# A scale and an offset read by GpSimd as one value for two neighbouring channels

## The chip, the cores and the metric

The kernel runs on one core of a Trainium2 chip. The metric is the device time of one execution in microseconds (us), as the median of several runs. In the profile, PE is TensorE's matmuls and PEld its weight loads, DVE is VectorE, ACT ScalarE, POOL GpSimd and SP SyncE, which here only issues transfers.

## The reference

Two layers of the same kind follow each other on an image of 512 x 512 positions with 64 channels, all in float32. Cut to what matters:

```python
def _gn(v, G=32, eps=1e-5):                 # 32 groups of two channels
    g = v.reshape(B_, H_, W_, G, C_ // G)
    m = jnp.mean(g, axis=(1, 2, 4), keepdims=True)
    s = jnp.var(g, axis=(1, 2, 4), keepdims=True)
    return ((g - m) / jnp.sqrt(s + eps)).reshape(v.shape)

def conv_ref(x, ...):                       # x is _gn of the layer's input
    xn = _ln(x, norm_scale, norm_bias)      # over the 64 channels
    left  = (xn @ Wl + bl) * mask * sigmoid(xn @ Wlg + blg)     # 64 -> 128
    right = (xn @ Wr + br) * mask * sigmoid(xn @ Wrg + brg)
    out_gate = sigmoid(xn @ Wog + bog)
    out = _banded_ingoing(left, right, 4)   # out[i] = sum over |d| <= 4 of left[i+d, i] * right[i+d]
    out = _ln(out, out_norm_scale, out_norm_bias) * out_gate
    return out @ Wo + bo                    # 128 -> 64

x = x + conv_ref(_gn(x), layer 0)
x = x + conv_ref(_gn(x), layer 1)
```

The first norm of a layer, `_gn`, has one mean and one variance for each group of two channels, over all positions. So it is one multiplier and one summand for each of 32 groups, the same at every position.

## The kernel before

Before the first layer the kernel reads the whole input once and takes its statistics (`input_stats`). The statistics of the second layer's input come from sums that the first layer takes on the way (`mid_stats`). Both end in `group_affine`, on VectorE, which makes the norm's multiplier `ga` and summand `gb`. Both are tiles of 128 partitions x 64 channels, the same on every partition, with each group's value written twice, once for each of its channels.

The image is worked on in nine blocks of rows; 64 rows of a block lie on the partitions, twice, for the left and the right half of the columns. A unit is eight columns of a block: its input tile `z` has 128 partitions x 8 columns x 64 channels, which is 512 contiguous values on a partition. Each unit goes through these steps, among others:

- `load` brings `z` from memory, through the SP queue.
- `scale` multiplies `z` by `ga` and `move` adds `gb`, in place. Both run on GpSimd, but for a few units at each layer's start that VectorE takes (`which`).
- `inner` takes the statistics of the second norm (`sti`) on VectorE; `centre` subtracts its mean and `resc` multiplies by its root (`rs`), both on GpSimd, in place. Here one value serves all 64 channels of a position.
- `ztr` transposes `z` on TensorE, into the PSUM tiles named `banks`; `keep`, `proj`, `sig` and `right` make the right factor `RO` from it.
- `band` multiplies the rows of `RO` with the band matrix `A` on TensorE and `copy` puts the result back into `RO`. `A` is loaded by the SP queue from `left_of`, anew for each block of rows.
- `ost` takes the statistics of the output norm, `norm` makes `on` from `RO`, part of the time on GpSimd (marked `!` in the tables) and else on ScalarE; `turn`, `gate`, `tg`, `last` and `end` finish the unit, and `stp` stores it.

The order of all this is written out by hand in two tables, `FIRST` and `SECOND`, one for each layer. A table is one period of eight units, called a chunk here; a layer has 36 chunks, four for each block of rows. Instructions that are recorded this way keep the order of the program on each engine, and all have line L492 in the profile, so groups are told apart by tile names.

`mid(v, n)` makes a view of a tile that repeats all its values n times, with a step of zero outside; `last(v, n)` repeats each value n times, with a step of zero inside. The scale reads `ga` through `mid`, the second norm's steps read theirs through `last`:

```python
engine.tensor_tensor(u.z, u.z, mid(ga, JU), ALU.mult)                   # scaled: 8 times 64 values
en.gpsimd.tensor_tensor(u.z, u.z, last(u.rs, D), ALU.mult)              # rescaled: 8 values, 64 times each
```

Of the kernel before, what the change touches and what calls it, by code (L numbers as in the profile page):

```python
# [10 lines left out]
F32 = mybir.dt.float32  # L11
# [3 lines left out]
ALU = mybir.AluOpType  # L15
# [4 lines left out]
P = 128  # L20
# [4 lines left out]
JU = 8  # L25
# [101 lines left out]
def mid(v: bass.AP, n: int) -> bass.AP:  # L127

    p, c = v.shape
    return v.unsqueeze(1).broadcast_to([p, n, c])  # L130
# [28 lines left out]
def tile_two_banded_layers(  # L159
# [6 lines left out]
    nc = tc.nc  # L166
# [3 lines left out]
    G = D // 2  # L170
# [3 lines left out]
    const = ctx.enter_context(tc.tile_pool(name="const", bufs=1))  # L174
# [62 lines left out]
    def rsqrt(o: bass.AP, v: bass.AP, sm):  # L237


        p, n = v.shape  # L240
        t, u = sm.tile([p, n], F32, name="rsqrt_t"), sm.tile([p, n], F32, name="rsqrt_u")
        nc.vector.tensor_scalar(
            o.bitcast(I32), v.bitcast(I32), -0.5, float(0x5F3759DF), ALU.mult, ALU.add
        )
        for a, b, c in ((1.0, -10.0 / 3.0, 5.0), (0.0, -27.0 / 1024.0, 0.5625)):
            nc.vector.tensor_tensor(t, o, o, ALU.mult)
            nc.vector.tensor_tensor(t, t, v, ALU.mult)
            nc.vector.tensor_scalar(u, t, a, b, ALU.mult, ALU.add)
            nc.vector.tensor_tensor(u, u, t, ALU.mult)
            nc.vector.tensor_scalar(u, u, c, None, ALU.add)  # L250
            nc.vector.tensor_tensor(o, o, u, ALU.mult)
# [144 lines left out]

    ga = const.tile([P, D], F32, name="ga")
    gb = const.tile([P, D], F32, name="gb")
    bo = [const.tile([P, D], F32, name="bo0"), None]
    bo_col = const.tile([P, 1], F32, name="bo_col")  # L400

# [6 lines left out]
    def group_affine(mean: bass.AP, var: bass.AP, pool):  # L408

        ve = pool.tile([P, D], F32, name="g_ve")  # L410
        nc.vector.tensor_scalar(ve, var, GN_EPS, None, ALU.add)
        rsqrt(ga, ve, pool)
        nc.vector.scalar_tensor_tensor(gb, mean, -1.0, ga, ALU.mult, ALU.mult)

    def input_stats(meanwhile, afterwards):
        flat = x.rearrange("h w c -> (h w) c").rearrange("(p n) c -> p n c", p=P)
# [3 lines left out]
        with tc.tile_pool(name="gnx", bufs=3) as gx, tc.tile_pool(name="gns", bufs=1) as gs:  # L420
# [23 lines left out]
            for t in range(n_t):  # L444
# [30 lines left out]
                vc.rearrange("p (g t) -> p g t", t=2), last(vg, 2), 0.5 / P, None, mult  # L475
            )
            group_affine(mc, vc, gs)


# [39 lines left out]
    def load_near(src: bass.AP, u: Unit):  # L519
# [3 lines left out]
        for o0, n0, n1 in spans:  # L523
            for o, r, k, m in runs(n0, n1):
# [20 lines left out]
                for q, g0, g1, a in pieces:  # L545
                    if g0 < g1:
# [2 lines left out]
                            strided(src, a * D, (D, 1), (1, (g1 - g0) * D)),  # L549
                        )  # L550

    def scaled(u: Unit, engine):
        engine.tensor_tensor(u.z, u.z, mid(ga, JU), ALU.mult)

    def moved(u: Unit, engine):
        engine.tensor_tensor(u.z, u.z, mid(gb, JU), ALU.add)

    def inner_stats(u: Unit, st: bass.AP, k: int):

# [356 lines left out]
    def layer(src: bass.AP, dst: bass.AP, w: dict, stats: bool, then=None):  # L916
# [57 lines left out]
        def on_scale(n, t, alt, b):  # L974
            for u in inputs(t):
                scaled(u, which(u, alt))

        def on_move(n, t, alt, b):
            for u in inputs(t):
                moved(u, which(u, alt))  # L980
# [155 lines left out]
    def mid_stats(sm):  # L1136
# [28 lines left out]
        nc.vector.tensor_scalar(var, var, 0.0, None, ALU.max)  # L1165
        nc.vector.tensor_tensor(ev[:, :D], ev[:, :D], bo[0], ALU.subtract)
        group_affine(ev[:, :D], var, sm)


# [95 lines left out]
def build(arrays):  # L1265
    import concourse.bacc as _bacc

    nc = _bacc.Bacc("TRN2", target_bir_lowering=False, num_devices=1)
    aps = {}
    for name in _INS:  # L1270
        a = arrays[f"in_{name}_dram"]
        aps[name] = nc.dram_tensor(
            f"in_{name}_dram", a.shape, mybir.dt.from_np(a.dtype), kind="ExternalInput"
        ).ap()
    out = nc.dram_tensor("out_0_dram", aps["x"].shape, F32, kind="ExternalOutput").ap()
    layers = [{n: aps[f"L{i}_conv_{n}"] for n in _NAMES} for i in range(2)]
    with tile.TileContext(nc) as tc:
        tile_two_banded_layers(tc, aps["x"], layers, out)
    return nc
# [10 lines left out]
```

## Time and profile before

| | |
|---|---|
| median of 3 runs | 4331.73 us (4329.06 to 4340.09) |
| span of the profiled execution | 4342.3 us |
| that span beside the median of the runs | 10.6 us longer; no time of that execution but its span is known |
| busy: PE, DVE, ACT, POOL | 3778.1, 3667.7, 3189.2, 3754.3 us |
| GpSimd's four instructions on `z`: by `ga`, by `gb`, by `sti`, by `rs` | 716.8, 715.7, 620.1, 614.9 us |
| GpSimd's `on<-RO,rs,nm` | 1129.1 us |

Busy time is time with an instruction at work; a share of the span is an average over stages. A group's row reads: line, engine, operation, output tile<-input tiles, their shapes, xcount, then busy us and mean ns of one, then the engine's idle time before them and what ended it. An idle time or a wait is put down to what came last.

### The profile page before, as it was taken

The numbers are of one execution on the slowest core, as the hardware profiler recorded it, in microseconds if no ns is written. First come the engines' busy times: TensorE is split into PE (matmuls) and PEld (weight loads), VectorE is DVE, ScalarE is ACT, GpSimd is POOL, SyncE is SP. The second block draws the span as 40 slices with busy tenths as digits, with TensorE's granted clock in tenths as the row PEclk, the third lists the DMA queues.
The fourth block names the chain that finished last, engine by engine and source line by source line (L and its number), as shares of the span: only waits on it lengthen the run. The fifth ranks groups of instructions, "written<-read, shape, count | busy, mean of one in ns | idle before, by whom it ended". The sixth has DMA issues, their size and how long they took to land.

```text
span 4342.3 us, 223298 instructions
## 1 busy us (share of the span) xinstructions
PE 3778.1 (87%) x94986; PEld 3263.8 (75%) x94986; DVE 3667.7 (84%) x9911; ACT 3189.2 (73%) x5976; POOL 3754.3 (86%) x4962
## 2 busy tenths in 40 slices
PE   0169899999898999999995889898989899989998
PEld 0058787878787878888874778787878787878786
DVE  8988787878787888888877788898989898989897
ACT  0048787878787877777773778787878787878787
POOL 2379898989898999999956789898989898989894
PEclk9989999999999999999997999999999999999999
DMA  9844545454545454445434344445454545454533
GB/s 393 313 110 108 134 113 143 115 141 114 140 115 138 112 141 120 131 123 129 125 109 114 101 136 124 139 128 138 123 142 122 143 120 145 121 145 121 152 112 100
DMA packets 695719, 596.26 MB, mean 137 GB/s; under 512 B 138310, under 2 KB 549990, under 8 KB 692420
## 3 DMA queue, kind: packets, MB, share of 16 engines
q1 hardware_dynamic: 692212, 580.43, 47.1%
q8 instruction: 748, 12.26, 1.2%
q14 instruction: 247, 2.02, 0.2%
q0 software_dynamic: 2512, 1.56, 0.1%
HBM read 436.71 MB, written 149.74 MB: 135 GB/s over the span
## 4 chain that ended last, share of the span: by engine, by line
PE 46%; POOL 20%; DVE 11%; DMA 9%; SPq 7%; issue 6%; ACT 2%; POOLq 0%; DVEq 0%; ACTq 0%
PE banks L492 35%; POOL z L492 13%; PE bank L492 8%; SPq L492 7%; POOL on L492 6%; PE acc L492 2%; DVE RO L492 2%; DMA z<-in_x_dram 2%; DMA z<-mid_x 2%; DVE gn_st L492 2%; DVE sti L492 1%; DVE sto L492 1%; DVE XR L492 1%; DVE ZH L492 1%; DMA raw<-in_L_conv_Wl_dram 1%
## 5 line engine op out<-in xcount | busy, mean ns | idle before, releaser
L492 POOL TENSOR_SCALAR on<-RO,rs,nm 128x128 f32<-128x128 f32 x2520 | 1129.1, 464 | 157.1 <-PE banks L492 111.2
L492 ACT ACTIVATE on<-RO,nm,rs 128x128 f32<-128x128 f32 x2088 | 971.2, 499 | 106.6 <-PE banks L492 95.2
L492 PE MATMUL banks<-pack,ZT 64*128 64x128 f32 x9216 | 992.3, 287 | 24.1 <-DVE RO L492 13.7
L492 PE MATMUL banks<-pack,zT 64*128 64x128 f32 x9216 | 953.1, 279 | 1.8 <-ACT zT L492 1.0
L492 POOL TENSOR_TENSOR z<-z,ga 128x512 f32<-128x512 f32 x556 | 716.8, 1296 | 261.0 <-DMA z<-mid_x 117.7
L492 ACT ACTIVATE sg<-banks 128x512 f32<-128x512 f32 x1170 | 696.6, 596 | 296.7 <-PE banks L492 270.9
L492 PEld LDWEIGHTS banks<-pack,ZT 64*128 64x128 f32 x9216 | 781.9, 194 | 148.4 <-DVE RO L492 47.5
L492 DVE TENSOR_TENSOR RO<-banks,sg 128x512 f32<-128x512 f32 x1152 | 777.3, 682 | 113.3 <-ACT sg L492 76.6
L492 DVE BATCH_NORM_STATS2 sto<-RO 128x6 f32<-128x256 f32 x2304 | 847.0, 413 | 5.2 <-ACT RO L492 4.0
L492 DVE SCALAR_TENSOR_TENSOR ZH<-banks,pack,ZH 128x896 f32<-128x896 f32 (+1 forms) x576 | 668.0, 1160 | 186.3 <-PE banks L492 155.4
L492 PEld LDWEIGHTS banks<-pack,zT 64*128 64x128 f32 x9216 | 762.2, 194 | 3.5 <-ACT zT L492 2.3
L492 PEld LDWEIGHTS banks<-RO,A 64*64 64x64 f32 x36864 | 617.7, 136 | 159.8 <-DVE RO L492 50.8
L492 PE MATMUL banks<-RO,A 64*64 64x64 f32 x36864 | 694.2, 223 | 48.6 <-issue 20.2
L492 POOL TENSOR_TENSOR z<-z,gb 128x512 f32<-128x512 f32 x556 | 715.7, 1293 | 3.3
L492 ACT COPY RO<-banks 128x1024 f32<-128x1024 f32 x540 | 539.8, 1008 | 194.5 <-PE banks L492 186.4
L492 PE MATMUL bank<-pack,ZH 128*64 128x64 f32 x18432 | 666.2, 226 | 15.7 <-DVE XR L492 5.6
L492 PEld LDWEIGHTS bank<-pack,ZH 128*64 128x64 f32 x18432 | 593.0, 139 | 76.7 <-issue 34.3
L492 ACT ACTIVATE ZH<-banks 128x896 f32<-128x896 f32 (+1 forms) x576 | 531.8, 930 | 142.6 <-PE banks L492 135.2
L492 POOL TENSOR_TENSOR z<-z,rs 128x512 f32<-128x512 f32 x586 | 614.9, 1059 | 19.7 <-DVE rs L492 19.4
L492 POOL TENSOR_TENSOR z<-z,sti 128x512 f32<-128x512 f32 x586 | 620.1, 1072 | 7.6 <-DVE sti L492 7.5
L492 DVE BATCH_NORM_STATS2 sti<-z 128x6 f32<-128x128 f32 x2344 | 505.6, 282 | 120.2 <-POOL z L492 118.0
L492 PE MATMUL banks<-ZT,pack 64*128 64x448 f32 (+1 forms) x2304 | 589.7, 584 | 9.8 <-DVE RO L492 5.5
(202 smaller groups left out, 4169.3 us busy)
## 6 DMA issues: line engine op xcount, KB each, us to landing
z<-in_x_dram SPq DMA_DIRECT2D x576, 128.0 KB
A<-left_of SPq DMA_DIRECT2D x576, 128.0 KB
z<-mid_x SPq DMA_DIRECT2D x576, 128.0 KB
gn_x<-in_x_dram SPq DMA_DIRECT2D x16, 4096.0 KB
XR<-in_x_dram SPq DMA_DIRECT2D x448, 112.0 KB
mid_x<-XR SPq DMA_DIRECT2D x448, 112.0 KB
XR<-mid_x SPq DMA_DIRECT2D x448, 112.0 KB
out_dram<-XR SPq DMA_DIRECT2D x448, 112.0 KB
```

Of the source, the lines that this page charges most:

```text
L492: return lambda *a, **k: tc.keep_in_program_order(f(*a, **k))
```

## The change

`group_affine` makes two more tiles, `ga2` and `gb2`, which hold one value for each of the 32 groups, by two copies on VectorE after `gb`. The scale and the offset then read those: a view with three dimensions after the partition, eight columns with step zero, 32 groups with step one, and two channels with step zero. The view of `z` is split the same way, which still is 512 contiguous values, and it is built as such. `ga` and `gb` stay.

```diff
+    ga2 = const.tile([P, G], F32, name="ga2")
+    gb2 = const.tile([P, G], F32, name="gb2")
...
         nc.vector.scalar_tensor_tensor(gb, mean, -1.0, ga, ALU.mult, ALU.mult)
+        for g, v in ((ga2, ga), (gb2, gb)):
+            nc.vector.tensor_copy(g, v.rearrange("p (g t) -> p g t", t=2)[:, :, 0])
...
+    def by_group(u: Unit, v: bass.AP, op, engine):
+
+        z = u.z.rearrange("p j (g t) -> p j g t", t=2)
+        engine.tensor_tensor(z, z, mid(v, JU).unsqueeze(3).broadcast_to([P, JU, G, 2]), op)
+
     def scaled(u: Unit, engine):
-        engine.tensor_tensor(u.z, u.z, mid(ga, JU), ALU.mult)
+        by_group(u, ga2, ALU.mult, engine)
 
     def moved(u: Unit, engine):
-        engine.tensor_tensor(u.z, u.z, mid(gb, JU), ALU.add)
+        by_group(u, gb2, ALU.add, engine)
```

The order of instructions is the same on every engine but for VectorE, which has the two copies at each layer's start. On VectorE at the first layer's start, from the summand on, before:

```order
L413 SCALAR_TENSOR_TENSOR gb<-gn_mc,ga 128x64
L492 TENSOR_TENSOR z<-z,ga 128x512
L492 TENSOR_TENSOR z<-z,gb 128x512
```

And now, where `ga_93` and `gb_94` are the tiles `ga2` and `gb2`, and lines further down have moved (L492 is L496):

```order
L415 SCALAR_TENSOR_TENSOR gb<-gn_mc,ga 128x64
L417 COPY ga_93<-ga 128x32
L417 COPY gb_94<-gb 128x32
L496 TENSOR_TENSOR z<-z,ga_93 128x512
L496 TENSOR_TENSOR z<-z,gb_94 128x512
```

The two copies stand between the summand and the first unit's scale, and nothing else has moved. GpSimd's first scale, which waited for `ga`, now waits for the copies.

## The prediction

> **What bounds the kernel now.** I read the head of the page first, then the stretches of single chunks, then the waits, and the groups by shape last, for prices.
>
> ```profile
> span 4342.3 us, 223298 instructions
> PE 3778.1 (87%) x94986; PEld 3263.8 (75%) x94986; DVE 3667.7 (84%) x9911; ACT 3189.2 (73%) x5976; POOL 3754.3 (86%) x4962
> PE 46%; POOL 20%; DVE 11%; DMA 9%; SPq 7%; issue 6%; ACT 2%; POOLq 0%; DVEq 0%; ACTq 0%
> ```
>
> Busy shares over the whole span name nobody: TensorE has 87%, GpSimd 86%, VectorE 84%. The chain that ended last (third line) has TensorE first and GpSimd second. So the question goes to single chunks. A chunk is eight units, one pass through the table of steps. I cut the stretches below where every eighth `z<-z,sti` of GpSimd starts. The columns are the length, then each engine's busy time.
>
> ```profile
> core 0: us, PE busy (x) PEld busy (x) DVE busy (x) ACT busy (x) POOL busy (x), PEclk, DMA share, GB/s
> 1027.10:1079.80 52.70, 51.17 (x1380) 44.97 (x1380) 46.13 (x125) 43.37 (x81) 52.62 (x71) 1.00 0.49 117
> 1132.50:1198.40 65.90, 54.95 (x1364) 48.44 (x1364) 45.30 (x119) 41.93 (x79) 52.74 (x71) 0.90 0.55 147
> 1478.50:1531.20 52.70, 51.16 (x1380) 45.00 (x1380) 46.06 (x125) 43.15 (x81) 52.62 (x71) 1.00 0.49 117
> 2151.10:2201.70 50.60, 50.37 (x1368) 44.43 (x1366) 42.69 (x106) 42.62 (x80) 41.47 (x62) 1.00 0.35 95
> 2528.00:2579.20 51.20, 50.74 (x1288) 43.73 (x1285) 48.58 (x131) 45.87 (x90) 50.17 (x65) 1.00 0.48 138
> 3072.80:3123.20 50.40, 49.54 (x1266) 42.87 (x1264) 47.05 (x127) 44.64 (x87) 50.15 (x66) 1.00 0.39 118
> 3225.30:3287.70 62.40, 52.88 (x1262) 45.53 (x1260) 47.24 (x126) 44.39 (x86) 50.18 (x66) 0.89 0.53 146
> 3718.20:3768.50 50.30, 49.27 (x1262) 42.48 (x1259) 46.74 (x126) 44.31 (x86) 50.02 (x65) 1.00 0.39 118
> ```
>
> In an ordinary chunk GpSimd is full: 52.62 of 52.70 us in the first layer, 50.02 of 50.30 and 50.15 of 50.40 in the second. It sets the period. TensorE is close behind, with 51.17 of 52.70 and 49.27 of 50.30: 1.5 us of slack a chunk in the first layer and 1.0 in the second. Its granted clock there is 1.00, so its busy time cannot shrink by a better clock. VectorE has 3.6 to 6.6 us of slack. Two chunks show what happens when TensorE is the bound: at 2151.10 us GpSimd has only 41.47 us of work and TensorE is busy 50.37 of 50.60, and at 2528.00 us it is 50.74 of 51.20. So a TensorE-bound chunk is its busy time plus 0.2 to 0.5 us.
>
> Every fourth chunk, where the next block of rows begins, is 62 to 66 us long. GpSimd's work is the same there; the rest is a stall.
>
> ```profile
> POOL z L492 <- DMA z<-mid_x: 117.7, 45, 14.0
> POOL z L492 <- DMA z<-in_x_dram: 107.1, 39, 5.5
> PE banks L492 <- POOL on L492: 120.3, 69, 5.8
> 3022.04 1.27 POOL L492 TENSOR_TENSOR z<-z,ga 128x512 f32<-128x512 f32 x1 [5.03 <-DMA z<-mid_x]
> 3009.94 1.15 SPq L492
> 3027.64 2.88 DMA z<-mid_x
> ```
>
> The first three lines are waits in all, times and the longest; the fourth is GpSimd in the stall at 3022 us; the last two are the first and the last piece of this part of the chain of waits. From 3009.94 to 3027.64 us, 17.7 us, the chain runs through the issuing of transfers on the SP queue, where the loads of `z` stand among those of `A`. A faster GpSimd does not shorten that piece.
>
> **What the change touches.** The order of instructions on all engines is the same but for four copies on VectorE. What changes is the second operand of the scale and the offset: 32 values, each read twice running, eight times over, where it was 64 values read once each, eight times over. The first operand and the result, `z`, stay 512 contiguous values. So nearly all hangs on the duration of one form. The nearest rows on GpSimd (busy us, mean ns, idle before):
>
> ```profile
> L492 POOL TENSOR_TENSOR z<-z,ga 128x512 f32<-128x512 f32 x556 | 716.8, 1296 | 261.0 <-DMA z<-mid_x 117.7 <-DMA z<-in_x_dram 107.1 <-PE banks L492 18.2
> L492 POOL TENSOR_TENSOR z<-z,gb 128x512 f32<-128x512 f32 x556 | 715.7, 1293 | 3.3
> L492 POOL TENSOR_TENSOR z<-z,rs 128x512 f32<-128x512 f32 x586 | 614.9, 1059 | 19.7 <-DVE rs L492 19.4
> L492 POOL TENSOR_TENSOR z<-z,sti 128x512 f32<-128x512 f32 x586 | 620.1, 1072 | 7.6 <-DVE sti L492 7.5
> L492 POOL TENSOR_TENSOR gn_s<-gn_s,gn_off 128x64 f32<-128x64 f32 x28 | 9.0, 320 | 2.1
> L492 POOL TENSOR_TENSOR gn_off<-gn_st 128x64 f32<-128x64 f32 x14 | 5.8, 414 | 40.6 <-DVE gn_st L492 40.6
> L492 POOL TENSOR_TENSOR gn_own<-gn_own,gn_st 128x64 f32<-128x64 f32 x14 | 4.7, 336 | 0.0
> L492 POOL TENSOR_SCALAR on<-RO,rs,nm 128x128 f32<-128x128 f32 x2520 | 1129.1, 464 | 157.1 <-PE banks L492 111.2 <-DVE nm L492 36.0 <-ACT acc L492 5.3
> masks.py:199 POOL TENSOR_SCALAR_AFFINE_SELECT ident<-ident 128x128 f32<-128x128 f32 x1 | 0.3, 323 | 0.1
> ```
>
> *Low end.* `z<-z,rs` and `z<-z,sti` have the same size, the same engine and the same contiguous `z`; their second operand repeats one value 64 times. They take 1059 and 1072 ns against 1296 and 1293. So repeating a value is worth up to 237 ns, and how far two repeats get of the way that 64 get is the unknown. *No gain:* 1296. *Above:* two rows have operands in runs of two. `gn_own<-gn_own,gn_st` reads its second operand as 32 runs of two, and takes 336 against the 320 of `gn_s`, all contiguous: 16 ns for 32 runs, 0.5 ns a run, and with 256 runs 128 ns on top of 1296, 1424 ns. `on<-RO` reads 64 runs of two, 1 KB apart, in 464 ns against the 323 of a contiguous one of that size: 2.2 ns a run, 564 ns for 256, 1860 ns. That row has another operation with two scalars read besides, so it is the farther.
>
> Between these I take the middle of 1296 and 1059, 1178 ns. The reason is in the `gn_` rows. With one operand strided the price is 16 ns, with both (`gn_off<-gn_st`, 414) it is 94. So the extra time seems to come where both operands go on to fresh memory together, not from either alone. `ga` and `z` now do so in step; with pairs, the second goes on half as often, so half of the 237 ns should go: 118 ns an instruction.
>
> [...]
>
> **The sum.** Per chunk 8 scales and 8 offsets: 16 × 118 ns = 1.89 us less on GpSimd. First layer: 52.62 − 1.89 = 50.73, below TensorE's 51.17, so TensorE sets the period: 51.17 + 0.35 (the middle of the two chunks above) = 51.5, a gain of 1.2 us. Second layer: 50.1 − 1.9 = 48.2, below TensorE's 49.4; 49.4 + 0.35 = 49.75 against 50.35, a gain of 0.6 us. A layer has 36 chunks; without the 8 at a change of block and some 3 at the ends, 25 are ordinary: 25 × 1.2 + 25 × 0.6 = 45 us. In the 16 chunks at a change of block all but the SP queue's piece is as elsewhere; two thirds of the mean gain of 0.9 us gives 16 × 0.6 = 10 us. Together 55 us. At a layer's end I count nothing (in the chunk at 2151.10 us GpSimd is not the bound), nor at its start, where ten such instructions in a row would be 1.2 us.
>
> The copies lie on the path at each layer's start, since all units wait for the scale:
>
> ```profile
> 213.01 0.22 DVE L413 SCALAR_TENSOR_TENSOR gb<-gn_mc,ga 128x64 f32<-128x64 f32 x1
> 213.06 1.29 POOL L492 TENSOR_TENSOR z<-z,ga 128x512 f32<-128x512 f32 x1 [17.66 <-DVE ga L251]
> 209.34 0.19 DVE L474 TENSOR_SCALAR gn_vc<-gn_vg 128x64 f32<-128x64 f32 x1
> 209.56 0.20 DVE L411 TENSOR_SCALAR g_ve<-gn_vc 128x64 f32<-128x64 f32 x1
> L492 DVE TENSOR_TENSOR z<-z,ga 128x512 f32<-128x512 f32 x30 | 33.9, 1144 | 6.3 <-DMA z<-mid_x 5.2 <-DMA z<-in_x_dram 1.1
> L492 DVE TENSOR_TENSOR z<-z,gb 128x512 f32<-128x512 f32 x30 | 31.2, 1050 | 0.2
> ```
>
> GpSimd starts right when `ga` is done, at 213.06. It will wait for `gb` (0.22 us) and, as bounded by the 0.19 and 0.20 us of 64-wide rows, two copies: 0.6 us a layer, 1.2 us in both. VectorE's own 60 scales and offsets change their operand too. L474 reads each value twice running, in 0.19 us, against 0.20 for the contiguous L411: no price either way. Nothing else is added, and nobody's queue order moves.
>
> So 55 − 1.2 = 54 us less. The profiled execution's span, 4342.3, is 10.6 us above the median of the runs, 4331.7; the difference is taken from the median: **4278 us**.
>
> How far this can be off while its mechanism holds: if the whole 237 ns went, TensorE would still be the bound, so the time is nearly the same; if TensorE packed closer than its busy time tells, GpSimd's 1112 instructions × 118 ns = 131 us would be the most, 4200. If TensorE's waits on ScalarE and VectorE grow as GpSimd's go, half is left, 4305. Its own range is 4240 to 4312.
>
> **The rivals.**
>
> *The form does not change its time (no change).* If GpSimd's price is per value fetched, with a run of two costing as much as two contiguous ones, it stays at 1296 ns and the time at 4332 + 1. The low row needs 64 repeats, and nothing shows what two are worth. It is also the outcome if the gain is there but TensorE, at 97 to 98% in ordinary chunks, gives none of its 1.0 to 1.5 us. Against: 1296 to 1059 is a step in just the property that the change uses.
>
> [...]
>
> *Runs of two cost more than they save (slower).* Place: the same 1112 instructions, in the engine that sets the period, so each ns is paid: 16 ns a chunk per ns, 1.1 us over the kernel. At 1424 ns, 128 × 1112 = 142 us more, 4474 us; at the far end, 1860 ns, 627 us more. It decides from 1296 + 12 ns on (12 × 1112 = 13 us). For it: `gn_own` is the nearest row with runs of two, and it is dearer than contiguous. Against: its runs are also strided, 12 bytes apart inside and 384 between, and the new ones lie side by side.
>
> **How the numbers follow.** Faster with TensorE as the new bound, 4278: 0.60. No change, by either way: 0.20. Slower: 0.20, most of it below 1424 ns, a twentieth at the far end. About 0.3%, 13 us, is what a measurement of this kernel can tell from no change. The range starts at 4235, leaving out a twentieth in which TensorE packs closer, and goes up to 4400, which holds no change and about the milder quarter of the slower cases (up to 60 ns an instruction); beyond it lie 0.15. As cases of both signs are in it, the likeliest one's own 4240 to 4312 stands beside it.
>
> **What would show it.** In the profile of the changed kernel: `z<-z,ga2` and `z<-z,gb2` near 1178 ns (right), at 1296 (first rival), above 1310 (second); `z<-z,rs` unchanged at 1059. In ordinary chunks GpSimd should show 1 us or more idle, first named as waiting for TensorE's `banks` or for `z` transfers, and TensorE within 0.5 us of the chunk's length, at 51.5 and 49.75 us. Chunks at a change of block should keep a stall of about 11 us. The prediction is wrong if GpSimd is faster and the chunks stay at 52.7 and 50.3, or if chunks get shorter than TensorE's busy time now.

## The result, and the profile after

The changed kernel takes 4286.2 us (median of 4 runs, 4281.05 to 4288.38) against 4335.9 for the kernel before (4 runs, 4329.06 to 4346.16). The ratio is 0.9886, with a 95% interval of 0.9870 to 0.9903: 1.1% faster, some 50 us. The two profiled spans differ by 4342.3 − 4286.6 = 55.7 us. The forecast was 4278.

The head of the page of the changed kernel, with the chain's shares by engine:

```profile
span 4286.6 us, 223301 instructions
PE 3756.5 (88%) x94986; PEld 3258.3 (76%) x94986; DVE 3657.6 (85%) x9915; ACT 3181.7 (74%) x5976; POOL 3620.0 (84%) x4962
PE 58%; DVE 12%; POOL 9%; DMA 7%; SPq 6%; issue 5%; ACT 2%; DVEq 0%; POOLq 0%; ACTq 0%
```

GpSimd's busy time fell by 134 us and its share of the chain from 20% to 9%; TensorE's rose from 46% to 58%. Where GpSimd's time went is seen in the groups by shape (the profile prints `ga` for `ga2`):

```profile
L496 POOL TENSOR_TENSOR z<-z,gb 128x512 f32<-128x512 f32 x556 | 651.5, 1177 | 3.3
L496 POOL TENSOR_TENSOR z<-z,ga 128x512 f32<-128x512 f32 x556 | 649.8, 1175 | 301.9 <-DMA z<-in_x_dram 135.3 <-DMA z<-mid_x 114.5 <-PE banks L496 20.0
L496 POOL TENSOR_TENSOR z<-z,sti 128x512 f32<-128x512 f32 x586 | 617.8, 1067 | 7.7 <-DVE sti L496 7.7
L496 POOL TENSOR_TENSOR z<-z,rs 128x512 f32<-128x512 f32 x586 | 611.9, 1053 | 20.9 <-DVE rs L496 20.5
```

The scale takes 1175 ns and the offset 1177, 121 and 116 ns less than before; the other two forms are as they were, within 6 ns. The stretches of single chunks, two of the first layer (the second one at a change of block), then three of the second (the last one at a change of block):

```profile
core 0: us, PE busy (x) PEld busy (x) DVE busy (x) ACT busy (x) POOL busy (x), PEclk, DMA share, GB/s
1466.50:1517.50 51.00, 49.90 (x1353) 44.18 (x1353) 45.55 (x122) 42.62 (x81) 50.70 (x71) 1.00 0.46 116
1127.50:1193.20 65.70, 54.83 (x1370) 48.49 (x1366) 44.92 (x117) 42.00 (x79) 50.64 (x70) 0.90 0.53 143
2624.00:2672.90 48.90, 48.84 (x1262) 42.52 (x1262) 46.91 (x127) 44.29 (x86) 48.16 (x66) 1.00 0.39 122
3464.10:3512.80 48.70, 48.60 (x1260) 42.27 (x1260) 46.57 (x126) 44.05 (x86) 48.09 (x65) 1.00 0.39 122
2772.70:2833.30 60.60, 51.05 (x1256) 43.97 (x1254) 46.85 (x126) 43.96 (x85) 48.30 (x66) 0.92 0.53 150
```

In the second layer's ordinary chunk TensorE is busy 48.84 of 48.90 us and 48.60 of 48.70, while GpSimd has 0.6 to 0.7 us to spare. In the first layer's chunk shown, GpSimd still has the larger busy time, 50.70 of 51.00, against 49.90 for TensorE.

A block of rows is four chunks. The means over eight blocks of each layer, from the starts of every eighth `z<-z,sti` in both traces, in us (for the last two rows the eight begin one block earlier, as those of the last block fall in the layer's end):

| chunk | layer 1 before | after | layer 2 before | after |
|---|---|---|---|---|
| at the change of block | 64.20 | 64.43 | 62.14 | 60.88 |
| the next | 52.81 | 51.60 | 50.34 | 49.02 |
| the one after | 52.77 | 51.73 | 51.18 | 49.87 |
| the last of the block | 54.73 | 54.63 | 51.08 | 49.73 |

Eight times the differences: 17 us less in the first layer, from two chunks of four; 42 us less in the second, from all four. Together they are 59 us; outside these chunks the execution became 59 − 55.7 = 3 us longer. Of the mean lengths in the second layer TensorE is busy 48.87 of 49.02, 49.16 of 49.87 and 49.20 of 49.73 us (before 49.39, 49.44 and 49.71), and GpSimd 48.2 of each. In the first layer's two chunks that became shorter, neither is full: TensorE is busy 50.70 of 51.60 and 50.94 of 51.73 us, GpSimd 50.75 and 50.76.

The waits in all, as before in us, times and the longest:

```profile
POOL on L496 <- PE banks L496: 139.9, 86, 7.3
POOL z L496 <- DMA z<-in_x_dram: 135.3, 44, 6.7
PE banks L496 <- POOL on L496: 119.3, 48, 5.7
POOL z L496 <- DMA z<-mid_x: 114.5, 52, 10.8
```

GpSimd's wait for the first layer's input grew from 107.1 to 135.3 us: that is the layer in which half of the chunks gave nothing back. The last row of `ga` on VectorE, in the kernel before and now, then the copies and GpSimd's first scale:

```profile
212.75 0.22 DVE L251 TENSOR_TENSOR ga<-ga,rsqrt_u 128x64 f32<-128x64 f32 x1
212.55 0.22 DVE L251 TENSOR_TENSOR ga<-ga,rsqrt_u 128x64 f32<-128x64 f32 x1
212.96 0.17 DVE L417 COPY ga<-ga 128x32 f32<-128x32 f32 x1
213.07 0.18 DVE L417 COPY gb<-gb 128x32 f32<-128x32 f32 x1
213.21 1.15 POOL L496 TENSOR_TENSOR z<-z,ga 128x512 f32<-128x512 f32 x1 [18.01 <-DVE ga L417]
```

`ga` was finished at 212.97 us and GpSimd's scale started at 213.06, 0.09 us later; now `ga` is finished at 212.77 and the scale starts at 213.21, 0.44 us later. So the copies cost 0.35 us here. The scale starts before the second copy is done (213.07 + 0.18 = 213.25): it waits for the first alone.

### The profile page after: what moved, and what is told of

Read it like the earlier page. It is cut to its first block, busy times and chain, and to the rows that moved or that the text cites. A ratio compares the mean times of both kernels' runs of the same rounds, so it can differ in the third digit from the quotient of the medians.

```text
span 4286.6 us, 223301 instructions
## 1 busy us (share of the span) xinstructions
PE 3756.5 (88%) x94986; PEld 3258.3 (76%) x94986; DVE 3657.6 (85%) x9915; ACT 3181.7 (74%) x5976; POOL 3620.0 (84%) x4962
## 4 chain that ended last, share of the span: by engine, by line
PE 58%; DVE 12%; POOL 9%; DMA 7%; SPq 6%; issue 5%; ACT 2%; DVEq 0%; POOLq 0%; ACTq 0%
PE banks L496 44%; PE bank L496 10%; POOL z L496 6%; SPq L496 6%; POOL on L496 3%; PE acc L496 3%; DVE sti L496 2%; DMA z<-in_x_dram 2%; DVE RO L496 2%; DVE sto L496 2%; DVE gn_st L496 2%; DMA z<-mid_x 2%; DVE XR L496 1%; DVE ZH L496 1%; ACT on L496 1%
## 5 line engine op out<-in xcount | busy, mean ns | idle before, releaser
L496 POOL TENSOR_SCALAR on<-RO,rs,nm 128x128 f32<-128x128 f32 x2520 | 1117.9, 456 | 193.3 <-PE banks L496 139.9
L496 ACT ACTIVATE on<-RO,nm,rs 128x128 f32<-128x128 f32 x2088 | 971.7, 499 | 108.4 <-PE banks L496 95.1
L496 PE MATMUL banks<-pack,ZT 64*128 64x128 f32 x9216 | 987.4, 287 | 24.4 <-DVE RO L496 15.3
L496 PE MATMUL banks<-pack,zT 64*128 64x128 f32 x9216 | 945.0, 279 | 2.2 <-issue 1.3
L496 POOL TENSOR_TENSOR z<-z,ga 128x512 f32<-128x512 f32 x556 | 649.8, 1175 | 301.9 <-DMA z<-in_x_dram 135.3
L496 ACT ACTIVATE sg<-banks 128x512 f32<-128x512 f32 x1170 | 696.1, 596 | 279.9 <-PE banks L496 253.8
L496 PEld LDWEIGHTS banks<-pack,ZT 64*128 64x128 f32 x9216 | 771.5, 194 | 148.4 <-DVE RO L496 49.6
L496 DVE TENSOR_TENSOR RO<-banks,sg 128x512 f32<-128x512 f32 x1152 | 777.6, 683 | 94.8 <-ACT sg L496 72.5
L496 DVE BATCH_NORM_STATS2 sto<-RO 128x6 f32<-128x256 f32 x2304 | 847.9, 413 | 6.7 <-ACT RO L496 2.6
L496 DVE SCALAR_TENSOR_TENSOR ZH<-banks,pack,ZH 128x896 f32<-128x896 f32 (+1 forms) x576 | 668.7, 1161 | 195.5 <-PE banks L496 163.2
L496 PEld LDWEIGHTS banks<-pack,zT 64*128 64x128 f32 x9216 | 754.0, 194 | 3.9 <-ACT zT L496 2.4
L496 PEld LDWEIGHTS banks<-RO,A 64*64 64x64 f32 x36864 | 617.2, 136 | 139.0 <-DVE RO L496 43.9
L496 PE MATMUL banks<-RO,A 64*64 64x64 f32 x36864 | 693.4, 223 | 32.3 <-issue 18.8
L496 PE MATMUL bank<-pack,ZH 128*64 128x64 f32 x18432 | 666.7, 226 | 12.5 <-DVE XR L496 5.6
L496 ACT COPY RO<-banks 128x1024 f32<-128x1024 f32 x540 | 540.2, 1008 | 173.6 <-PE banks L496 162.1
L496 POOL TENSOR_TENSOR z<-z,gb 128x512 f32<-128x512 f32 x556 | 651.5, 1177 | 3.3
L496 PEld LDWEIGHTS bank<-pack,ZH 128*64 128x64 f32 x18432 | 594.0, 139 | 72.9 <-issue 31.0
L496 ACT ACTIVATE ZH<-banks 128x896 f32<-128x896 f32 (+1 forms) x576 | 531.6, 929 | 135.2 <-PE banks L496 129.4
L496 POOL TENSOR_TENSOR z<-z,rs 128x512 f32<-128x512 f32 x586 | 611.9, 1053 | 20.9 <-DVE rs L496 20.5
L496 POOL TENSOR_TENSOR z<-z,sti 128x512 f32<-128x512 f32 x586 | 617.8, 1067 | 7.7 <-DVE sti L496 7.7
L496 PE MATMUL banks<-ZT,pack 64*128 64x448 f32 (+1 forms) x2304 | 587.3, 583 | 3.4 <-issue 1.2
L496 PE MATMUL banks<-ident,on 64*128 64x64 f32 x9216 | 461.7, 230 | 125.7 <-POOL on L496 119.3
```

Source lines behind the costliest of these rows:

```text
L496: return lambda *a, **k: tc.keep_in_program_order(f(*a, **k))
```

## The experiments

Two things were open: why the instruction got faster, and what limits the kernel now. The experiments ran on chips on which the kernel before took 4350 to 4354 us, so times are compared as ratios to it; the changed kernel's, 0.9886, is from the runs above, and it was not run on these chips.

### Why the instruction is faster

Three theories of the author's: V, every fresh value of the second operand costs; O, every new stretch of memory that it enters costs; J, this costs only where the first operand enters one at the same element. The prediction rested on J without showing it. How long a stretch would be, no run shows.

Pairs without the compact tiles:

```diff
-    ga2 = const.tile([P, G], F32, name="ga2")
+    ga2 = ga.rearrange("p (g t) -> p g t", t=2)[:, :, 0]
```

> The scale and the offset read pairs straight out of ga and gb: 32 values two apart (8 bytes), each read twice running; no compact tiles and no copies. So there are as few fresh values as in the changed kernel, but the second operand goes through as many bytes as before. If the price is for each fresh value of the second operand (theory V), GpSimd's instruction takes 1177 ns as in the changed kernel and the time is 4286. [...] If runs of two had a price of their own, hidden in the changed kernel, it is above 1296.

```profile
L494 POOL TENSOR_TENSOR z<-z,ga 128x512 f32<-128x512 f32 x556 | 714.7, 1293 | 271.6 <-DMA z<-in_x_dram 114.8 <-DMA z<-mid_x 110.0 <-DVE ga L251 32.4
```

1293 ns, as before; the ratio is 1.0002 (0.9991 to 1.0012). Reading half as many values is worth nothing; keeping them close together is what counts. V falls; O and J fit, as the operand goes through as many bytes as before. Runs of two have no price of their own either, since this form has them too.

The kernel before, its tiles moved by 8 bytes (`gb` likewise), so that by J, if a stretch is longer than that, the two operands no longer enter one at the same element:

```diff
-    ga = const.tile([P, D], F32, name="ga")
+    ga = const.tile([P, D + 8], F32, name="ga")[:, 2 : D + 2]
```

> [...] Theory J: the two never enter together, so the price is gone: 1059 ns, the level of z<-z,rs, and a time of 4275 to 4286, set by TensorE. Theories O and V: nothing changes for the second operand, 1296 ns and 4332.

```profile
L492 POOL TENSOR_TENSOR z<-z,ga 128x512 f32<-128x512 f32 x556 | 612.6, 1108 | 347.0 <-DMA z<-in_x_dram 160.2 <-DMA z<-mid_x 156.4 <-DVE ga L251 17.7
```

1108 ns from 1296, with the same values read in the same pattern, from another place. O falls, J fits, but for some 50 ns that stay above 1059. The ratio is 0.9891 (0.9865 to 0.9918): the whole gain of the change, without its tiles, copies and view.

The changed kernel, its tiles moved by 4 bytes (`ga2 = const.tile([P, G + 8], ...)[:, 1 : G + 1]`, and `gb2`), to the same end:

> [...] Theory J: 1059 ns, against 1177 unshifted; as TensorE sets the period already, the time falls by 10 us at most, 4275 to 4286. Theories O and V: 1177 ns and 4286.

```profile
L496 POOL TENSOR_TENSOR z<-z,ga 128x512 f32<-128x512 f32 x556 | 611.1, 1105 | 334.1 <-DMA z<-in_x_dram 155.6 <-DMA z<-mid_x 116.2 <-DVE ga L417 33.1
```

1105 ns from 1175: as J has it, with the same rest above 1059. The ratio is 0.9878 (0.9860 to 0.9896), no different from the changed kernel's, though each instruction is 70 ns shorter.

Each value for four channels (`"p (g t) -> p g t", t=4`, tiles of 16 values):

> Each value is read for four neighbouring channels (16 values instead of 32, the first of each four, so the first norm's result is another). All three theories: a quarter of the 237 ns is left, 1059 + 59 = 1118 ns. The time is set by TensorE: 4275 to 4286. If instead the step from 1296 to 1177 had another cause than the share of fresh values, such as the number of dimensions of the view, it stays at 1177.

```profile
L496 POOL TENSOR_TENSOR z<-z,ga 128x512 f32<-128x512 f32 x556 | 617.3, 1116 | 327.6 <-DMA z<-in_x_dram 156.3 <-DMA z<-mid_x 122.9 <-PE banks L496 27.2
```

1116 ns where 1118 was expected: in tiles that are not moved the price goes with the share of entries, all to 1296 ns, a half to 1175, a quarter to 1116. The ratio is 0.9887 (0.9864 to 0.9910).

The kernel before, moved by 4 bytes in place of 8 (`[:, 1 : D + 1]`):

> [...] Theory J as e2 left it: anything but together is free of the price, so 1107 ns as there. If the price fades with the distance between the two entries, it is between 1107 and 1296.

```profile
L492 POOL TENSOR_TENSOR z<-z,ga 128x512 f32<-128x512 f32 x556 | 611.7, 1107 | 331.3 <-DMA z<-in_x_dram 156.0 <-DMA z<-mid_x 133.3 <-DVE ga L251 32.4
```

1107 ns: one value's distance does as well as two. Its single run took 4298 us beside 4350, about the same ratio. What the last 45 to 50 ns are is not settled: if they were for the second operand's own entries, they should have halved from `e2` to `e3`, and they did not. Two things stay open with them. The three moved forms take 1105 to 1108 ns whatever they read, which also fits a flat time for any second operand that does not start where such a stretch does, with a price for its own entries in the other forms alone; a run with `z` moved as well would tell, and there is none. And under J the moves by 4 and 8 bytes show only that a stretch is longer than 8 bytes, not how long it is.

### What limits the kernel now

Half the edit (the offset reads `gb` as before):

```diff
-        by_group(u, gb2, ALU.add, engine)
+        engine.tensor_tensor(u.z, u.z, mid(gb, JU), ALU.add)
```

> Only the scale reads pairs; the offset reads gb as before. GpSimd then wins half, 8 x 118 ns = 0.95 us a chunk: 51.7 us of work in the first layer, 49.2 in the second, just at TensorE's 51.2 and 49.3. If TensorE takes over as the prediction has it, half of the edit brings most of the gain: 0.9 us a chunk in the first layer and 0.6 in the second, some 40 to 45 us with the chunks at a change of block, a ratio of 0.990. Rival: the time follows GpSimd's work all the way, and the whole edit is only worth 55 us because some of each saved us is lost in waits; then half the edit is worth half, 27 us, a ratio of 0.9937.

The ratio is 0.9937 (0.9922 to 0.9953), the rival's number to the digit. Up to half the edit the time still follows GpSimd's work, at the rate that the whole edit has.

All of it and more, one value for 64 channels:

```diff
-        engine.tensor_tensor(z, z, mid(v, JU).unsqueeze(3).broadcast_to([P, JU, G, 2]), op)
+        engine.tensor_tensor(u.z, u.z, last(v[:, :JU], D), op)
```

> The scale and the offset read one value for all 64 channels of a column, as rs is read (so the first norm's result is another). GpSimd: 1059 ns an instruction, 3.8 us less a chunk than before, twice the changed kernel's gain. If TensorE is the bound after the change, the time is that of the changed kernel or up to 10 us below: a ratio of 0.986 to 0.989. If GpSimd's work still sets it: 0.976.

```profile
L496 POOL TENSOR_TENSOR z<-z,ga 128x512 f32<-128x512 f32 x556 | 587.5, 1062 | 362.5 <-DMA z<-in_x_dram 173.0 <-DMA z<-mid_x 140.8 <-DVE ga L417 33.2
```

```profile
2630.60:2679.20 48.60, 48.59 (x1258) 42.23 (x1256) 46.67 (x126) 44.09 (x87) 46.42 (x66) 1.00 0.40 123
```

1062 ns an instruction and a ratio of 0.9883 (0.9867 to 0.9899): twice the saving on GpSimd, and nothing more for the kernel. In the chunk shown GpSimd has 46.42 us of work in 48.60, and TensorE 48.59. So the saving pays up to the changed kernel's level and stops there: GpSimd's work is no longer what limits the kernel.

More work for TensorE, first in the kernel before, then in the changed one:

```diff
-        for e in range(2):
+        for e in (0, 1) * (2 if o.at % NU == 3 else 1):      # in gates
```

> The kernel before, with the gate's matmuls (banks<-ZT,pack, four records in 0.85 us) done twice for one unit of eight, into the same bank with the same result: TensorE gets 0.85 us more a chunk. If GpSimd is the bound there and TensorE has 1.5 us of slack in the first layer and 1.0 in the second, this is hidden: 0 to 15 us, a ratio of 1.000 to 1.0035.

> The same 0.85 us more a chunk for TensorE in the changed kernel. If TensorE is the bound there, as the prediction has it, it is paid in the second layer's 36 chunks and in the half of the first layer's that had become shorter (the others wait for transfers): 36 x 0.85 + 18 x 0.85 = 46 us, a ratio of 0.9992 where the changed kernel has 0.9886. Rival, after the run without the seeds brought nothing: waits or transfers limit the changed kernel and TensorE still has slack; then as in the kernel before, 0 to 15 us, 0.989 to 0.992.

The changed kernel goes to 0.9985 (0.9970 to 1.0000), 0.0099 × 4350 = 43 us more, close to the 46 of a TensorE that is full. The kernel before goes to 1.0062 (1.0046 to 1.0077), 27 us more where 15 was the most expected: less of its slack was usable than busy times show. The same work costs more in the changed kernel, as it must if TensorE is nearer to its limit there; by the intervals the difference is 16 us, give or take 12. By the traces, 34 us of it lie in the second layer, where the chunk after a change of block is 49.60 us long with TensorE busy for 49.53.

Less work for TensorE, in both kernels (`seeded` not called, `end(outs[t], w, True)`):

> The kernel before without the second layer's seeding matmuls, bank<-pieces,ones, which add the output bias of both layers (left out here); the first matmul on the bank starts the sum instead. This takes TensorE 8 matmuls a chunk of 0.21 us each, 1.7 us in 36 chunks. If GpSimd is the bound of the kernel before, its chunks in the second layer stay at 50.3 us and the time falls by 5 us at most, a ratio of 0.999 or more. If TensorE were the bound, by 40 to 60 us.

> The changed kernel without the same matmuls. If TensorE is its bound, the second layer's chunks fall to what GpSimd needs, 48.15 + 0.15 = 48.3 us from 48.7 to 50, and those at a change of block by as much: 25 x 1.1 + 8 x 1 = 35 us below the changed kernel, a ratio of 0.980 to the kernel before, where the changed kernel has 0.9886. Rival: what limits the changed kernel is not TensorE's work but the waits between engines or the transfers; then it stays at 0.987 to 0.989.

The kernel before stays, 0.9993 (0.9983 to 1.0004). The changed one stays too, 0.9886 (0.9869 to 0.9902), where 0.980 was expected: a miss. A seed adds much less to TensorE's busy time than its record's 0.38 us, and less than the 0.21 us expected, a distance seen in the changed kernel from the start of a seed to that of the next matmul (3045.70 and 3045.91 us): others overlap with it. The timeline of the kernel before, a seed and the transposes that start with it:

```profile
3104.78 0.38 PE L492 MATMUL bank<-pieces,ones 64*128 64x512 bf16 x1
3104.78 0.49 PE L492 MATMUL banks<-ident,on 64*128 64x64 f32 x6
```

And a chunk of the changed kernel without seeds:

```profile
2635.40:2684.20 48.80, 48.20 (x1252) 41.37 (x1250) 46.59 (x126) 44.16 (x86) 48.20 (x65) 1.00 0.40 122
```

TensorE's busy time is 0.4 to 0.6 us less than in the chunks shown above, for eight seeds, not 1.7, and the chunk is no shorter, with TensorE and GpSimd both at 48.20 of 48.80. The means of eight agree: in the chunk after a change of block TensorE is busy 48.46 us in place of 48.87, and the chunk takes 49.12 us in place of 49.02. Had this been paid back in some 33 chunks, it would have been 14 us, little more than the two intervals can tell (10 us). So the run took away too little to test the bound well, but what it shows is on the rival's side: with TensorE's busy time alone lowered, nothing is won. What fills the last 0.6 us, when two engines are both that close to the chunk's length, is open.

### The stall at a change of block

In the changed kernel, `A` loaded by half as many transfers (one over `k` in place of two):

```diff
-        q = HA // 4
+        q = HA // 2
...
-            for k in range(2):
```

> The changed kernel, with A's loads for a new block of rows issued as 16 transfers of twice the rows in place of 32. On the SP queue an issue of A takes 0.65 us, and in the stall at a change of block five groups of four stand between the loads of z. If it is the issuing that sets this stall, as the prediction says, five groups become 1.3 us shorter each: 6.5 us for each of 16 changes of block, 104 us, a ratio of 0.965. If the stall is set by the transfers themselves, or by what they wait for, nothing changes: 0.9886. Between them if an issue of twice the rows takes longer than 0.65 us.

On the SP queue, one group of loads of `A` and the loads of `z` behind it in the changed kernel:

```profile
2987.81 2.58 SPq L496 DMA_DIRECT2D A<-left_of  x4
2990.50 1.63 SPq L496 DMA_DIRECT2D z<-mid_x  x2
```

and with half the transfers:

```profile
2939.53 1.28 SPq L496 DMA_DIRECT2D A<-left_of  x2
2940.92 1.21 SPq L496 DMA_DIRECT2D z<-mid_x  x2
```

An issue takes the same 0.64 us for twice the rows, so a group is 1.3 us shorter, as expected. The ratio is 0.9764 (0.9749 to 0.9780): 0.0122 × 4350 = 53 us below the changed kernel, half of the 104. By the means of eight, the chunk at a change of block fell from 64.43 to 58.04 us in the first layer, the 6.4 us that were expected, and from 60.88 only to 60.58 in the second. The chain in a stall of the second layer, by line, first in the changed kernel (2775 to 2805 us):

```profile
by line: PE banks L496 41.6%; SPq L496 27.9%; DMA z<-mid_x 9.6%; POOL z L496 7.5%; PE bank L496 6.7%; issue 4.1%; POOL on L496 2.9%; POOLq L496 0.1%
```

and with half the issues (2724 to 2760 us):

```profile
by line: DMA z<-mid_x 34.7%; PE banks L496 32.0%; POOL z L496 14.4%; POOL on L496 6.1%; PE bank L496 5.3%; SPq L496 4.5%; issue 3.4%; POOLq L496 0.1%
```

The windows are 30 and 36 us long, so the SP queue's part went from 8.4 to 1.6 us, and that of the transfers of `z` from 2.9 to 12.5 us: the stall is as long, with the transfers in the queue's place. In the changed kernel this stall is one with a small part for the queue. In the mean of the eight chunks at a change of block of the second layer, the queue's part of the chain went from 15.2 to 4.7 us, that of the transfers of `z` from 2.9 to 8.1 and that of the other transfers from 0.3 to 4.2. In the first layer the queue's part was 7.6 us and is 3.0, and the transfers of `z` have 8.9 and 10.9. Why the chain waits longer for transfers with half the issues is not shown. This version is the fastest of all here, 2.4% below the kernel before.

## Why the prediction was right, and where not

- **The instruction.** Forecast 1178 ns, measured 1175 and 1177. The reasoning from the `gn_` rows, that the price lies where both operands go on together, is borne out by `e1`, `e2`, `e3` and `e12`, but for the 45 to 50 ns that stay and the flat time for a moved operand that is not excluded. That half of the 237 ns should go was the author's estimate; 121 and 116 ns went.
- **The first rival**, that a run of two costs as much as two values, is excluded as stated: the form did get faster. But `e1` shows that no time would have been won if the pairs had been read from `ga` itself.
- **The second rival**, dearer runs of two, is excluded by the 1293 ns of `e1`, which has the same runs.
- **TensorE takes over.** Half shown. That GpSimd's work no longer limits is shown: `e2`, `e3`, `e4` and `e8` save 1.5 to 2 times as much on GpSimd for the same kernel time. That TensorE is nearer to its limit is shown by `e10`, which pays 43 us of the 46 expected, where 0.85 us in all 72 chunks would be 61. That TensorE's busy time alone is the bound is not shown: `e7` came out as its rival has it, and in the first layer TensorE had 0.8 to 0.9 us to spare, where the prediction wanted it within 0.5 us of the chunk. Nor is the limit the sharp one of the sum. By that, half the edit should have brought 40 to 45 us; it brought 27 (20 to 34 by its interval).
- **The split over the layers** was wrong, and that the total came so near is in part luck: two errors cancelled. The sum had 30 us from the first layer's ordinary chunks, 15 from the second's and 10 from the changes of block. Measured were 17 and 42 in all, in one trace of each kernel.
- **The ordinary chunks of the second layer** gained 1.3 us each, where 0.6 was forecast. Two steps failed. For the chunk after a change of block it is "its busy time cannot shrink by a better clock", taken as a floor of 49.4 us: at the same granted clock of 1.00 TensorE's busy time fell from 49.39 to 48.87 us in the mean of eight, and the chunk from 50.34 to 49.02, not 49.75. The prediction named chunks shorter than that busy time as what would make it wrong, and in this step it was. With as many matmuls in both traces, such a busy time seems to hold some waiting, here 0.5 us a chunk. For the other two kinds the end was right, 49.87 and 49.73 us, and the start was not: they took 51.18 and 51.08 us, and the sum had 50.35 for all three, from two chunks that both follow a change of block.
- **The ordinary chunks of the first layer** were the error the other way. Their new length of 51.5 us was right for two kinds (51.60 and 51.73), but 25 of 36 were counted, with 1.2 us each, and only these 16 got it. The last chunk of each block waits for transfers of `z` too, 2.6 us in the mean now, and kept its length.
- **The changes of block**, 0.6 us for each of 16, were mis-sized in both directions: nothing in the first layer, 1.26 us in the second. That the stall itself would stay is right: GpSimd is idle for 13.7 and 12.7 us there, where 11 were forecast. That the SP queue's issuing makes up 6.4 us of it in the first layer is shown by `e11`. In the second layer the chain runs through the queue for 15.2 us in the mean, as the prediction read it, but the transfers are right behind.
- **The copies** cost 0.35 us at the first layer's start, not 0.6: the first scale waits for one copy, which stands behind the summand on VectorE, and these rows overlap (the copy starts at 212.96 us, the summand ends at 213.03). At the second layer's start the scale comes 0.62 us after `ga` where it was 0.52.
- **A reading.** VectorE's slack in ordinary chunks, given as 3.6 us at the least, is 50.40 − 47.05 = 3.35 us in one of the lines shown; nothing hangs on it.

## What to carry to other kernels

When two engines are both near the length of a period, a saving on one can pay until the other is nearly full and then stop: here twice the saving on GpSimd (`e8`) gave a ratio of 0.9883 where the change gave 0.9886. Which one has the slack is better tried by adding work to each than read off busy times, since a busy time seems to hold waiting, here 0.5 us of 49.4 a chunk. Before a sum takes one chunk for all, see whether the others are as long. Before an operand is made smaller, try it from another place: moving two tiles by 8 bytes gave all of this gain (0.9891) with no new instruction. Where a stall runs through a queue that issues transfers, count the issues: one transfer of twice the rows cost the queue the same 0.64 us as one of half.

## What was not expected of the hardware

GpSimd's instruction with two inputs of 128 x 512 values depends on where the second lies: 1296 ns with its tile as allocated, 1108 with it moved by 8 bytes, 1107 by 4. The prediction had the idea, but not that a move alone would bring more than the pairs do.
